# Summing a head's exponentials: the two halves of j added on GpSimd before TensorE sums them

## The chip, the core and the metric

The kernel runs on one core of a Trainium2 chip. The metric is the device time of that core in microseconds (us), the median of several runs. All data are fp32.

## The reference, cut to what matters

Two layers work on 64 graphs of 256 nodes with 256 features. Layer 0 is two graph attention layers, a layer norm, a feed-forward part and another layer norm. Layer 1 is a relational attention with 8 heads of 32 features, then a feed-forward part. The change touches only the attention of layer 1:

```
scores = einsum('bhid,bhjd->bhij', q, k) / sqrt(dh)
attn   = softmax(scores, axis=-1)              # over j
out    = sum over r of einsum('bhij,bhjd->bhid', attn * (adj == r), v_r)
```

Since adj holds only 0 and 1 here, the kernel uses the relations 0 and 1 alone. It computes exp(scores) without taking a maximum away, multiplies by the values, sums exp over j beside that, and divides at the end.

## The kernel before, in words

The 64 graphs are worked on as 32 pairs. `whole_way(pair)` is a generator that goes through the stages of one pair: `gat_layers`, `feed_forward` with Relu, `attention`, `feed_forward` with Gelu, and the store. `in_turn` (L151) drives three such generators at once while the program is written. At each `yield us, later, needs` it counts a planned time on, and picks the next generator that is due by it. So the order of the instructions on every engine is fixed when the program is built, by the planned costs in the yields; on the chip each engine works through its own queue in that order and waits on semaphores.

In `attention` (L345) a graph b of the pair and a half c of the features make a group: four heads (HQ = 4) of 32 features, 4 groups for a pair, n = 0 to 3. For a group:

- `scores` (L354) makes exp(scores) transposed: j lies on the partitions, in two halves jc of 128, and i along the columns. The four heads' products (L360) use four row strips of TensorE. One exp per head (L365, ScalarE) writes the tile `a`, 128 x 512, that holds jc = 0 in its first 256 columns and jc = 1 in the other 256.
- `of_relation_1` (L369) multiplies `a` by adj into `m` on VectorE (L374), four times. `m` has 6 buffers for the 4 in use.
- `sums` (L378) multiplies `ones` (128 x 32) with `a` on TensorE (L381): for each half jc and each head o, 256 columns, adding the two halves up in PSUM. Its result, the sum over j for each i, lies on 32 partitions a head, in columns 256 to 511 of the bank `po`.
- `products` (L384) does the same with the values, once with `a` (r = 0) and once with `m` (r = 1), into columns 0 to 255 of `po` (L388).
- `divided` (L392) takes the reciprocal of the sums (L394), a check value (L396), and multiplies into `oT` (L398), all on VectorE.

The loop is software-pipelined: a step n first issues the scores of group n + 1 on TensorE, then the sums and products of group n, then on VectorE the m of group n + 1 and the division of group n. Between steps `in_turn` places a step of another pair, in this stage one block of the feed-forward part (L308). After n = 1 the values of the second graph are made (L335, L337). After n = 2 `into_rows(0)` projects the first graph (L405) and follows with `add_rows` (L266) and `layernorm` (L273 to L282) on VectorE; `into_rows(1)` comes after n = 3, with L319 blocks of another pair ahead of it. The layer norm has one instruction on GpSimd, the power that makes rstd (L276). GpSimd also adds a bias to the rows (L292) while they are transposed (L289, L290). On VectorE, `most` of a coming pair's adj (L216) lies among these.

A matmul of this kernel shows as two records in the profile[...].

Of the kernel before, what the change touches and what calls it, by code (L numbers as in the profile page):

```python
# [10 lines left out]
F32 = mybir.dt.float32  # L11
# [4 lines left out]
ALU = mybir.AluOpType  # L16
AX = mybir.AxisListType

P = 128
# [10 lines left out]
def two_layers(ctx: ExitStack, tc: tile.TileContext, t: dict, out: bass.AP, flag: bass.AP):  # L30
# [9 lines left out]
    nc = tc.nc  # L40
    B, N, D = out.shape
# [6 lines left out]
    DH = D // H  # L48
    HQ = P // DH
# [25 lines left out]
    ones = const.tile([P, DH], F32, name="ones")  # L75
# [28 lines left out]
    with tc.tile_pool(name="setup", bufs=1) as setup, \  # L104
# [11 lines left out]
        for m in range(KC):  # L116
            pw = psetup.tile([P, 512], F32, name="pw")
            for c in range(KC):
                nc.tensor.matmul(pw[:, :D + 4], lhsT=w1T[:, c, m * P:(m + 1) * P], rhs=right[:, c],
                                 start=c == 0, stop=c == KC - 1)  # L120
# [17 lines left out]
    work = ctx.enter_context(tc.tile_pool(name="work", bufs=1))  # L138
# [3 lines left out]
    def bank():  # L142
        return psum.tile([P, 512], F32, name="ps")
# [30 lines left out]
    def done_with(name):  # L174
        del alone[name]

    def of_graph(b):
        return slice(2 * b, 2 * b + 2)
# [84 lines left out]
    def add_rows(y, p, b):  # L263

        rows = y[:, of_graph(b), :].rearrange("p k d -> p (k d)")
        nc.vector.tensor_tensor(rows, p, rows, ALU.add)  # L266

    def layernorm(r, gb, b):
        g, beta = gb
        st, mv = small.tile([P, 2, 6], F32, name="st"), small.tile([P, 2, 2], F32, name="mv")  # L270
        rstd = small.tile([P, 2], F32, name="rstd")
        for j in range(2):
            nc.vector.bn_stats(st[:, j, :], r[:, 2 * b + j, :])  # L273
            nc.vector.bn_aggr(mv[:, j, :], st[:, j, :])
        nc.vector.tensor_scalar(rstd, mv[:, :, 1], EPS, None, ALU.add)  # L275
        nc.gpsimd.tensor_tensor(rstd, rstd, mhalf[:, :2], ALU.pow)  # L276
        for j in range(2):
            row = r[:, 2 * b + j, :]
            nc.vector.scalar_tensor_tensor(row, row, mv[:, j, 0:1], g, op0=ALU.subtract, op1=ALU.mult)
        for j in range(2):  # L280
            row = r[:, 2 * b + j, :]
            nc.vector.scalar_tensor_tensor(row, row, rstd[:, j:j + 1], beta, op0=ALU.mult, op1=ALU.add)  # L282
# [11 lines left out]
    def rows_transposed(y, bias):  # L294
        yT = work.tile([P, KC, 512], F32, name="yT", bufs=2)
        for b in range(2):
            transposed(y, yT, bias, b)
            yield 0.5, 0.5 + b * 0.5, None
        return yT
# [31 lines left out]
    def values(v, jc, at, yT):  # L331

        ps = bank()
        for c in range(KC):
            nc.tensor.matmul(ps, lhsT=yT[:, c, at:at + P], rhs=wv[:, c].rearrange("p r m -> p (r m)"),  # L335
                             start=c == 0, stop=c == KC - 1)
        nc.vector.tensor_tensor(v[:, jc], ps, bv, ALU.add)  # L337

    def projected(to, c, yT, w, bias, scale):
        ps = bank()  # L340
        for d in range(KC):
            nc.tensor.matmul(ps, lhsT=w[:, d, c * P:(c + 1) * P], rhs=yT[:, d, :], start=d == 0, stop=d == KC - 1)  # L342
        nc.scalar.activation(to[:, c, :], ps, AF.Identity, bias=bias[:, c:c + 1], scale=scale)

    def attention(y, pair, adjT):  # L345


        yT = yield from rows_transposed(y, bo)
        qT, kT, oT = (work.tile([P, KC, 512], F32, name=n) for n in ("qT", "kT", "oT"))

        def values_tile():
            return work.tile([P, 2, 2 * D], F32, name="v", bufs=2)

        def scores(b, c):  # L354
            ps = [bank() for _ in range(HQ)]
            for jc in range(2):
                at = b * N + jc * P
                for o in range(HQ):
                    rows = slice(o * DH, (o + 1) * DH)
                    nc.tensor.matmul(ps[o][:, jc * N:(jc + 1) * N], lhsT=kT[rows, c, at:at + P],  # L360
                                     rhs=qT[rows, c, b * N:(b + 1) * N], start=True, stop=True)
            e = []
            for o in range(HQ):
                a = work.tile([P, 512], F32, name="a", bufs=2 * HQ)
                nc.scalar.activation(a, ps[o], AF.Exp)  # L365
                e.append(a)
            return e

        def of_relation_1(b, e):  # L369
            adj = adjT[:, of_graph(b), :].rearrange("p k n -> p (k n)")  # L370
            ms = []
            for a in e:
                m = work.tile([P, 512], F32, name="m", bufs=HQ + 2)
                nc.vector.tensor_tensor(m, a, adj, ALU.mult)  # L374
                ms.append(m)
            return ms

        def sums(e, po):  # L378
            for jc in range(2):
                for o in range(HQ):  # L380
                    nc.tensor.matmul(po[o * DH:(o + 1) * DH, N:], lhsT=ones, rhs=e[o][:, jc * N:(jc + 1) * N],  # L381
                                     start=jc == 0, stop=jc == 1)

        def products(c, r, v, ms, po):  # L384
            for jc in range(2):
                for o in range(HQ):
                    at = r * D + (c * HQ + o) * DH
                    nc.tensor.matmul(po[o * DH:(o + 1) * DH, :N], lhsT=v[:, jc, at:at + DH],  # L388
                                     rhs=ms[o][:, jc * N:(jc + 1) * N],
                                     start=r == 0 and jc == 0, stop=r == 1 and jc == 1)  # L390

        def divided(b, c, po):  # L392
            s = work.tile([P, N], F32, name="s", bufs=2)
            nc.vector.reciprocal(s, po[:, N:])  # L394
            junk = work.tile([P, N], F32, name="junk")
            nc.vector.scalar_tensor_tensor(junk, po[:, N:], 1.0, s, op0=ALU.mult, op1=ALU.add,  # L396
                                           accum_out=reach[:, pair, b * KC + c:b * KC + c + 1])
            nc.vector.tensor_tensor(oT[:, c, b * N:(b + 1) * N], po[:, :N], s, ALU.mult)  # L398

        def into_rows(b):  # L400
            ps = bank()
            for j in range(2):
                k = 2 * b + j
                for c in range(KC):
                    nc.tensor.matmul(ps[:, j * D:(j + 1) * D], lhsT=oT[:, c, k * P:(k + 1) * P], rhs=wo[:, c, :],  # L405
                                     start=c == 0, stop=c == KC - 1)
            add_rows(y, ps, b)
            layernorm(y, ln[2], b)

        groups = [(b, c) for b in range(2) for c in range(KC)]  # L410
        v = values_tile()
        projected(qT, 0, yT, wq, bqs, SCALE)
        projected(kT, 0, yT, wk, bk, 1.0)
        yield 3.44, 0.0, None
        values(v, 0, 0, yT)
        yield 1.72, 0.0, None
        e = scores(*groups[0])
        ms = of_relation_1(0, e)
        projected(qT, 1, yT, wq, bqs, SCALE)
        yield 3.0, 0.0, None  # L420
        projected(kT, 1, yT, wk, bk, 1.0)
        values(v, 1, P, yT)
        yield 3.44, 0.0, None
        for n, (b, c) in enumerate(groups):
            last = n == len(groups) - 1
            if not last:
                ahead = scores(*groups[n + 1])
            po = bank()
            sums(e, po)
            products(c, 0, v, e, po)  # L430
            products(c, 1, v, ms, po)
            if not last:
                e, ms = ahead, of_relation_1(groups[n + 1][0], ahead)
            divided(b, c, po)
            yield 3.1 if last else 4.1, 3.2 if last else 0.8, None
            if (b, c) == (0, KC - 1):
                v = values_tile()
                for jc in range(2):
                    values(v, jc, N + jc * P, yT)
                    yield 1.72, 0.0, None  # L440
            if n == 2:
                into_rows(0)
                yield 1.75, 0.0, None
        into_rows(1)
        done_with("attention")
        yield 1.75, 4.5, "ff"

    def whole_way(pair):
        yield 0.0, 0.0, "gat"
        xT, adjT, x = loaded.pop(pair)  # L450
        yield from gat_layers(pair, xT, adjT, x)
        yield from feed_forward(x, ff0, AF.Relu, ln[1])
        yield 3.44, 4.5, "attention"
        yield from attention(x, pair, adjT)
        yield from feed_forward(x, ff1, AF.Gelu, ln[3])
        nc.sync.dma_start(out[2 * pair:2 * pair + 2].rearrange("b (c p) d -> p (b c) d", p=P), x)
        yield 3.44, 0.0, None
# [439 lines left out]
```

## Time and profile before

| what | us |
|---|---|
| median of 3 runs (3450.34 to 3454.68) | 3452.26 |
| the profiled execution's own time | 3450.98 |
| its span | 3449.2 |
| TensorE busy | 3344.4 (97%) |
| VectorE busy | 1904.6 (55%) |
| ScalarE busy | 1371.0 (40%) |
| GpSimd busy | 481.5 (14%), of it 206.1 the power of rstd and 276.1 the bias adds |
| sums with ones (L381), 2048 records | 137.0, 385 ns each |
| products with values (L388), 4096 records | 267.8, 379 ns each |
| m (L374), 512 | 327.0, 688 ns by the page, 686 at the median |
| exp (L365), 512 | 264.4, 602 ns by the page |
| bias add on GpSimd (L292), 384 | 728 ns at the median of the first feed-forward's |

The span of the profiled execution is 1.8 us shorter than its own time; what lies around it is start and end of the program. Matmul records overlap: four that run side by side each show 379 ns, so the time that a block of matmuls takes is read from the start of one block to the start of the next, not from the sum of its records. The granted clock of TensorE is full almost throughout (0.999).

### The profile page before, as it was taken

To read this page: it belongs to the slowest core of one execution; us is meant where nothing else is said; L and a number is where in the kernel's file an instruction comes from. 1 tells how busy PE (TensorE), PEld (TensorE's weight loads), DVE (VectorE), ACT (ScalarE), POOL (GpSimd) and SP (SyncE) were. 2 spreads that over 40 slices of the span, in tenths; PEclk is the share of its full clock that TensorE was granted. 3 is DMA by queue.
4 is the path that set the end of the run, shared out by engine and by line. 5 is a ranking of instruction groups with operands and counts; after the bars stand their busy time and mean duration, and the time that the engine had idled before them with its cause. 6 is when DMAs were issued, how large, how long until landed. Compare 5 with 4: busy or idle time off the path is not lost.

```text
span 3449.2 us, 47284 instructions
## 1 busy us (share of the span) xinstructions
PE 3344.4 (97%) x18698; PEld 2150.5 (62%) x18698; DVE 1904.6 (55%) x4825; ACT 1371.0 (40%) x2586; POOL 481.5 (14%) x646
## 2 busy tenths in 40 slices
PE   7999999999999999999999999999999999999998
PEld 5566665666656566565665666656666566565655
DVE  5655645556456564555645555465554655546455
ACT  4343343433434334343444434444253442534332
POOL 0201111011110111111111111111111111111110
PEclk9999999999999999999999999999999999999999
DMA  5000010000100001000000100001000010000000
GB/s 166 7 25 19 13 37 7 25 19 13 37 7 25 25 7 37 7 28 23 20 25 7 41 10 25 19 7 43 7 25 19 7 43 7 25 19 1 13 1 14
DMA packets 66868, 78.22 MB, mean 23 GB/s; under 512 B 3280, under 2 KB 57680, under 8 KB 66640
## 3 DMA queue, kind: packets, MB, share of 16 engines
q1 hardware_dynamic: 66640, 75.13, 7.0%
q8 instruction: 150, 2.46, 0.3%
q14 instruction: 78, 0.64, 0.1%
HBM read 58.34 MB, written 16.78 MB: 22 GB/s over the span
## 4 chain that ended last, share of the span: by engine, by line
PE 87%; ACT 9%; DVE 2%; DMA 1%; issue 0%; SPq 0%; POOL 0%; POOLq 0%; DVEq 0%
PE ps L319 26%; PE ps L308 23%; PE ps L342 7%; PE ps L335 6%; PE ps L388 6%; PE ps L360 4%; PE ps L381 4%; PE ps L253 3%; PE ps L405 3%; ACT L189 2%; ACT yT L290 2%; PE ps L241 2%; PE ps L227 2%; PE ps L289 1%; ACT ff L311 1%; DVE e L206 1%
## 5 line engine op out<-in xcount | busy, mean ns | idle before, releaser
L276 POOL TENSOR_TENSOR rstd<-rstd,mhalf 128x2 f32<-128x2 f32 x256 | 206.1, 805 | 2729.3 <-DVE rstd L275 2713.4
L308 PE MATMUL ps<-yT,w_L_gnn_W 128*128 128x512 f32 x1024 | 482.7, 602 | 14.2 <-ACT yT L290 12.5
L308 PE MATMUL ps<-yT,w_L_gnn_w_ff 128*128 128x512 f32 x1024 | 482.5, 602 | 14.1 <-ACT yT L290 12.5
L319 PE MATMUL ps<-w_L_gnn_w_ff,ff 128*128 128x256 f32 x2048 | 450.2, 379 | 0.0
L319 PE MATMUL ps<-w_L_gnn_W,ff 128*128 128x256 f32 x2048 | 449.9, 379 | 0.0
L319 PEld LDWEIGHTS ps<-w_L_gnn_W,ff 128*128 128x128 f32 x2048 | 389.1, 190 | 66.6 <-issue 15.3
L319 PEld LDWEIGHTS ps<-w_L_gnn_w_ff,ff 128*128 128x128 f32 x2048 | 389.0, 190 | 66.0 <-issue 14.8
L374 DVE TENSOR_TENSOR m<-a,adjT 128x512 f32<-128x512 f32 x512 | 327.0, 688 | 175.6 <-ACT a L365 134.9
L266 DVE TENSOR_TENSOR x<-ps,x 128x512 f32<-128x512 f32 x256 | 176.1, 688 | 444.3 <-PE ps L319 330.7
L311 ACT ACTIVATE ff<-ps,c_L_gnn_b_ff 128x512 f32<-128x512 f32 x256 | 176.0, 687 | 448.2 <-PE ps L308 448.2
L365 ACT ACTIVATE a<-ps 128x512 f32<-128x512 f32 x512 | 264.4, 602 | 216.3 <-PE ps L360 216.1
L337 DVE TENSOR_TENSOR v<-ps,b_L_gnn_bv 128x512 f32<-128x512 f32 x128 | 88.1, 689 | 400.5 <-PE ps L335 400.5
L308 PEld LDWEIGHTS ps<-yT,w_L_gnn_W 128*128 128x128 f32 x1024 | 183.0, 190 | 199.2 <-issue 174.1
L308 PEld LDWEIGHTS ps<-yT,w_L_gnn_w_ff 128*128 128x128 f32 x1024 | 183.1, 190 | 198.9 <-issue 174.2
L290 ACT ACTIVATE yT<-ps 128x512 f32<-128x512 f32 x192 | 110.2, 592 | 479.8 <-PE ps L289 479.8
L311 ACT ACTIVATE ff<-ps,c_L_gnn_b 128x512 f32<-128x512 f32 x256 | 175.9, 687 | 292.8 <-PE ps L308 292.4
L335 PE MATMUL ps<-wv,yT 128*128 128x512 f32 x512 | 235.4, 592 | 0.0
L229 ACT ACTIVATE xw<-ps 128x260 f32<-128x260 f32 x128 | 45.7, 379 | 456.0 <-PE ps L227 456.0
L394 DVE RECIPROCAL s<-ps 128x256 f32<-128x256 f32 x128 | 224.0, 1750 | 0.0
L273 DVE BATCH_NORM_STATS2 st<-x 128x6 f32<-128x256 f32 x512 | 192.7, 418 | 8.6
L206 DVE SCALAR_TENSOR_TENSOR e<-ps,ratio,up 128x256 f32<-128x256 f32 x256 | 115.7, 475 | 141.2 <-ACT up L201 141.2
L335 PEld LDWEIGHTS ps<-wv,yT 128*128 128x128 f32 x512 | 97.3, 190 | 122.5 <-issue 122.2
(81 smaller groups left out, 4290.1 us busy)
## 6 DMA issues: line engine op xcount, KB each, us to landing
xT<-in_xT SPq DMA_DIRECT2D x32, 512.0 KB, 4.6
adjT<-in_adjT SPq DMA_DIRECT2D x32, 512.0 KB, 3.9
x<-in_x SPq DMA_DIRECT2D x32, 512.0 KB, 4.2
out<-x SPq DMA_DIRECT2D x32, 512.0 KB, 3.2
w_L_gnn_w_ff<-in_L_gnn_w_ff SPq DMA_DIRECT2D x2, 1024.0 KB, 11.3
w_L_gnn_W<-in_L_gnn_W SPq DMA_DIRECT2D x2, 1024.0 KB, 7.0
wv<-in_L_gnn_Wv SPq DMA_DIRECT2D x2, 256.0 KB, 7.1
w_L_gnn_W1T<-in_L_gnn_W1T SPq DMA_DIRECT2D x1, 256.0 KB, 6.1
```

The source lines that it names most:

```text
L273: nc.vector.bn_stats(st[:, j, :], r[:, 2 * b + j, :])
L276: nc.gpsimd.tensor_tensor(rstd, rstd, mhalf[:, :2], ALU.pow)
L290: nc.scalar.activation(yT[:, :, b * N:(b + 1) * N], pt.rearrange("p (c n) -> p c n", c=KC), AF.Copy)
L308: nc.tensor.matmul(p1, lhsT=w1[:, c, m * P:(m + 1) * P], rhs=yT[:, c, :], start=c == 0, stop=c == KC - 1)
L311: nc.scalar.activation(h, p1, func, bias=b1[:, m:m + 1])
L319: nc.tensor.matmul(p2[:, j * D:(j + 1) * D], lhsT=f[m][:, k * P:(k + 1) * P], rhs=w2[:, m, :], start=m == 0, stop=m == NF - 1)
L335: nc.tensor.matmul(ps, lhsT=yT[:, c, at:at + P], rhs=wv[:, c].rearrange("p r m -> p (r m)"), start=c == 0, stop=c == KC - 1)
L342: nc.tensor.matmul(ps, lhsT=w[:, d, c * P:(c + 1) * P], rhs=yT[:, d, :], start=d == 0, stop=d == KC - 1)
L365: nc.scalar.activation(a, ps[o], AF.Exp)
L374: nc.vector.tensor_tensor(m, a, adj, ALU.mult)
L388: nc.tensor.matmul(po[o * DH:(o + 1) * DH, :N], lhsT=v[:, jc, at:at + DH], rhs=ms[o][:, jc * N:(jc + 1) * N], start=r == 0 and jc == 0, st ...
L394: nc.vector.reciprocal(s, po[:, N:])
```

## The change

`halves_added` is new: for each head of a group one GpSimd instruction adds the two halves of `a`, columns 0 to 255 and 256 to 511, into a tile `halves` of 128 x 256 with 6 buffers. `sums` then multiplies `ones` with that tile, one product a head instead of two. `products` still uses `a` itself. The planned costs of the steps in the loop are 0.4 lower.

```diff
+        def halves_added(e):
+            hs = []
+            for a in e:
+                h = work.tile([P, N], F32, name="halves", bufs=HQ + 2)
+                nc.gpsimd.tensor_tensor(h, a[:, :N], a[:, N:], ALU.add)
+                hs.append(h)
+            return hs
...
-        def sums(e, po):
-            for jc in range(2):
-                for o in range(HQ):
-                    nc.tensor.matmul(po[o * DH:(o + 1) * DH, N:], lhsT=ones, rhs=e[o][:, jc * N:(jc + 1) * N],
-                                     start=jc == 0, stop=jc == 1)
+        def sums(hs, po):
+            for o in range(HQ):
+                nc.tensor.matmul(po[o * DH:(o + 1) * DH, N:], lhsT=ones, rhs=hs[o], start=True, stop=True)
...
         e = scores(*groups[0])
-        ms = of_relation_1(0, e)
+        hs, ms = halves_added(e), of_relation_1(0, e)
...
             po = bank()
-            sums(e, po)
+            sums(hs, po)
             products(c, 0, v, e, po)
             products(c, 1, v, ms, po)
             if not last:
-                e, ms = ahead, of_relation_1(groups[n + 1][0], ahead)
+                e, hs, ms = ahead, halves_added(ahead), of_relation_1(groups[n + 1][0], ahead)
             divided(b, c, po)
-            yield 3.1 if last else 4.1, 3.2 if last else 0.8, None
+            yield 2.7 if last else 3.7, 3.2 if last else 0.8, None
```

## The prediction

> **What bounds the kernel now.** I read the page's totals and chain first, then the attention stage by itself: a window table over it, the waits of TensorE in it, and the timelines of TensorE and VectorE side by side.
>
> ```profile
> PE 3344.4 (97%) x18698; PEld 2150.5 (62%) x18698; DVE 1904.6 (55%) x4825; ACT 1371.0 (40%) x2586; POOL 481.5 (14%) x646
> ...
> PE 87%; ACT 9%; DVE 2%; DMA 1%; issue 0%; SPq 0%; POOL 0%; POOLq 0%; DVEq 0%
> ```
>
> TensorE is busy 97% of the span and is 87% of the chain; GpSimd is idle for six sevenths of it. In the stage that is changed TensorE has no gap at all. The row of the window table below (columns: stretch, its length, busy time of each engine) is the attention of one pair:
>
> ```profile
> 1597.00:1640.00 43.00, 43.00 (x333) 22.66 (x332) 27.05 (x48) 14.33 (x25) 1.10 (x2) 1.00 0.05 14
> ```
>
> So time taken off TensorE here is worth its full length until another engine comes last. Which one that would be is read from the two timelines (start, length, instruction, count). TensorE first, the last group of scores of a pair to its second output projection (L405):
>
> ```profile
> 1687.70 1.15 PE L360 MATMUL ps<-qT,kT 32*128 32x256 f32 x16
> 1688.78 1.07 PE L381 MATMUL ps<-a,ones 128*32 128x256 f32 x16
> 1689.67 1.05 PE L388 MATMUL ps<-a,v 128*32 128x256 f32 x16
> 1690.53 1.05 PE L388 MATMUL ps<-m,v 128*32 128x256 f32 x16
> ...
> 1695.15 1.07 PE L381 MATMUL ps<-a,ones 128*32 128x256 f32 x16
> ...
> 1703.15 1.03 PE L405 MATMUL ps<-w_L_gnn_Wo,oT 128*128 128x256 f32 x4
> ```
>
> and VectorE in the same stretch:
>
> ```profile
> 1689.50 1.29 DVE L374 TENSOR_TENSOR m<-a,adjT 128x512 f32<-128x512 f32 x2 [0.99 <-ACT a L365]
> 1691.66 1.29 DVE L374 TENSOR_TENSOR m<-a,adjT 128x512 f32<-128x512 f32 x2 [0.87 <-PE ps L388]
> 1692.88 1.75 DVE L394 RECIPROCAL s<-ps 128x256 f32<-128x256 f32 x1
> ...
> 1695.35 0.68 DVE L266 TENSOR_TENSOR x<-ps,x 128x512 f32<-128x512 f32 x1
> ...
> 1700.46 1.75 DVE L394 RECIPROCAL s<-ps 128x256 f32<-128x256 f32 x1
> ...
> 1702.59 0.42 DVE L398 TENSOR_TENSOR oT<-ps,s 128x256 f32<-128x256 f32 x1
> ```
>
> From the masked products m at 1689.50 to the last oT at 1702.59 + 0.42 = 1703.01, VectorE works through a queue with hardly a hole: four m, the division of group 3 (n = 2), L266 with the layer norm, then the division of group 4 (n = 3). The L405 block that starts at 1703.15 needs that oT from its second product on (the weights are taken chunk by chunk), at 1703.15 + 0.43 = 1703.58. The slack is 0.57 us, and the same to within 0.2 us in the pairs from 2 to 27. This is the nearest thing to a second bound.
>
> **What the Trainium skill says.** "TensorE: Matmul & The Clock Gate", Part 3 (packing small matmuls): products with 32 output columns on different column strips run side by side. The trace agrees: L388's 16 records take 0.86 us from block to block, four waves of 0.215. "SBUF — State Buffer", Who interferes with whom: GpSimd uses VectorE's second port pair; a VectorE operation with two SBUF inputs and a GpSimd operation that reads SBUF exclude each other. The trace agrees (columns: shortest/median/longest ns):
>
> ```profile
> L279 DVE SCALAR_TENSOR_TENSOR x<-x,mv,b_L_gnn_g_ln x256: 465/474/1029, 36.6 to 3349.5; 128x256 f32<-128x256 f32 x128
> L292 POOL TENSOR_TENSOR x<-x,b_L_gnn_b_ff x128: 714/728/1042, 42.0 to 3285.8; 128x256 f32<-128x256 f32 x128
> ```
>
> L279 has two SBUF inputs; it takes 474 ns alone and up to 1029 beside L292; L292 stretches from 728 to about 920. Statistics and PSUM reads on VectorE keep their length beside L292. "GPSIMD Engine Reference", Elementwise, puts a two-input add at 2.6 cycles an element, an estimate of 555 ns for 256 elements before dispatch; L292, the same operation on the same size, takes 728, and I use that.
>
> **The change, part by part.**
>
> *Removed:* per group, 8 of the 16 records of the sums, two of their four waves: 2 x 0.215 = 0.43 us (the sums take 0.89 us from start to next start now, 0.46 after). 32 pairs x 4 groups x 0.43 = 55 us, on the path.
>
> *Order:* the built programs of both kernels have the same order on ScalarE and VectorE, and on TensorE but for one L308 product of the first pair that changes places with L405's. The planner's smaller costs (3.7 for 4.1) move nothing else, so table loads stay. On GpSimd the 16 adds of a pair stand together, between a rstd power ahead and a rstd power behind; the power behind belongs to L266's layer norm, after the adds are done. SP's queue is as before.
>
> *Added:* 512 adds x 0.728 = 373 us on GpSimd, which goes from 14% to about 25%: no bound as a sum. The new buffers (6 for 4 in use) wait on sums of the group before, which TensorE does directly after the scores: free.
>
> *The new wait:* sums, first of a group's products, now wait for four adds, not for four exps; behind them in TensorE's queue stand all products. The exps of a group end 0.49 us apart. m and adds start on the same exps and both read two SBUF operands, so they take turns. The price of a turn: at 93.87 two L282 (two SBUF inputs, 256 wide) and three L292 alternate, and the two L282 that take 0.88 together alone take 1.82; their ends, and so a turn, are 0.88 us apart. m is 512 wide, 688 ns against 420 for 256 (L374, L398), so a turn of m and add is 0.88 + 0.27 = 1.15 us. Counted from the first m (1.80 us after the scores start), the fourth m ends after 0.69 + 3 x 1.15 = 4.13 us, the fourth add about 0.6 later, at scores + 6.5.
>
> When are the sums due? Scores to sums is 7.50, 6.79, 10.23 and 7.44 us for a pair's four groups. All but the first lose one shortened block, 0.43 (the third two): due at 7.50, 6.36, 9.4 and 7.01. Only the second group is late, by about 0.2 us. 32 x 0.2 = 6 us.
>
> *VectorE's queue:* in the fourth group the fourth m now ends at 1689.50 - 1687.70 + 4.13 = 5.93 us after the scores, against 1692.95 - 1687.70 = 5.25 before. From there to oT is unbroken VectorE work, 1703.01 - 1692.95 = 10.06 us, so oT comes at 15.99. TensorE wants it at 1703.58 - 1687.70 - 2 x 0.43 = 15.02, since two shortened blocks lie between. With some 0.05 us for the semaphore, L405 waits 1.0 us. In the last four pairs, where no next pair's adjT is reduced on VectorE (L216, 1.22 us), the slack is 1.3 us larger, and it doesn't wait. So 28 x 1.0 = 28 us come back. The first division in the pair also ends about 1 us later; its oT has 6 us to spare at the first L405, but the values' additions (L337) behind it may come to the third group's products with nothing to spare: 0.1 us a pair, 3 us.
>
> *Sum:* -55 + 6 + 28 + 3 = -18 us from the profiled 3450.98 (span 3449.2). The median of the runs shown is 3452.26, 1.3 us above that; from it, 3434 us.
>
> *Bounds of the unknown.* How m and add share is not in this trace for 512-wide operands. Lower end, m passing undisturbed: the fourth m, held by m's buffers until the products before are done, gains the same 0.43 and ends at 4.8; L405 is then due within 0.1 us of oT, and the whole 55 us stays less 3 at most: 3400. Two m ahead of the first add: fourth m at 5.4, wait 0.5, 28 x 0.5 + 9 = 23 back: 3420. The add first: fourth m at 6.4, wait 1.5, no late sums: -55 + 42 + 3 = -10, 3442. Upper end, the add holding the port for its whole 0.73 us: next rivals. I take turns with m first: both are released by the same exp, and L292's 728 ns against L374's 688 for half the elements leaves GpSimd the longer way to its first read (a guess; no row shows a tie).
>
> **Rivals.**
>
> *Full gain.* Adds fall into VectorE's waits for exps and for m's buffers (0.9 us holes at 1689 and 1691), and into its divisions, which read PSUM. For it: TensorE at 43.00 of 43.00. Against it: the adds become ready with the m. 3398 to 3424.
>
> *Slower: the port is the bound.* Each add holds the port for all of its 0.73 us and m runs at its 0.60 pitch: a turn of 1.33. The fourth m then ends at 1.80 + 0.69 + 3 x 1.33 = 6.48, L405 waits 1.5 us; the second group's fourth add ends at 1.80 + 4 x 1.33 + 0.1 = 7.2 against 6.36, and TensorE stands 0.85 us at the sums. 28 x (2.35 - 1.73) + 4 x (0.85 - 1.73) = +14 us; 3466, to 3480 if the values come late too. It decides once the two waits of a pair exceed 1.73 us. For it: GpSimd's 728 ns and L279's 1029. Against it: L282/L292's turn of 0.88, shorter than 0.39 + 0.73.
>
> *No change:* a turn near 1.25, or the add first with some late sums: 3445 to 3459.
>
> **How the numbers follow.** Turns as computed, 3425 to 3445: 0.48. Full gain or nearly: 0.17. No change: 0.15. Slower: 0.20. Bounds at 0.2% of 3452 are 3445 and 3459 (about what a measurement of this kernel can tell from no change). Faster 0.65, same 0.15, slower 0.20. The range leaves out half of the first rival and half of the slower one: 3408 to 3466. Both signs are possible; the likeliest case alone is 3425 to 3445.
>
> **What would show it.** In the profile after: the sums at 0.46 us a block and with half of L381's 137 us busy; adds of 0.73 to 0.95 us on GpSimd; m with a mean above 688 ns, near 950; a new TensorE wait of about 1.0 us at L405 for oT in 28 pairs, and one of 0.2 us at the second group's sums for the adds. No wait at L405 and m at 688 would mean the full gain. It is wrong if the sums wait in groups other than the second, if the order of a turn is not one each, or if other stages move, which this working leaves alone.

## The result, and the profile after

| | median us | runs | ratio to before | 95% interval |
|---|---|---|---|---|
| before | 3454.22 | 6 (same chip) | 1 | |
| after | 3455.55 | 6 (3453.92 to 3457.52) | 1.0007 | 0.9994 to 1.0019 |

No change can be measured. The forecast was 3434; the range (3408 to 3466) holds the result, the direction does not. The profiled execution of after took 3456.74 us, its span is 3455.0, the clock 0.998.

In after, lines 369 onward are shifted: the adds are L373, m is L382, the sums L388, the products L394, the reciprocal L400, oT L404, and the output projection L411. These are the page's totals, its chain, and the groups of the adds and of m (busy us, mean ns, idle before):

```profile
PE 3320.8 (96%) x17674; PEld 2131.0 (62%) x17674; DVE 2090.0 (60%) x4825; ACT 1368.5 (40%) x2586; POOL 1066.6 (31%) x1158
...
PE 74%; DVE 11%; ACT 9%; issue 3%; DMA 1%; POOL 1%; SPq 0%; ACTq 0%; DVEq 0%; POOLq 0%
...
L373 POOL TENSOR_TENSOR halves<-a 128x256 f32<-128x256 f32 x512 | 576.2, 1154 | 483.4 <-ACT a L365 483.4
L382 DVE TENSOR_TENSOR m<-a,adjT 128x512 f32<-128x512 f32 x512 | 517.9, 1070 | 104.3 <-ACT a L365 104.0
```

TensorE is 74% of the chain, not 87%, and VectorE 11%, not 2%. VectorE has the same 4825 instructions and is busy 185 us longer; m alone takes 191 us more, at 1070 ns each against 688. The adds take 1154 ns, where the same operation alone takes 728. So both engines pay for working at once. A stretch like the one shown of before, the attention of a pair beside a Relu feed-forward:

```profile
1602.00:1646.00 44.00, 43.27 (x308) 22.82 (x307) 32.58 (x48) 14.33 (x25) 19.02 (x18) 1.00 0.04 13
```

TensorE now stands still for 0.73 us in it, and VectorE works 32.6 of 44 us where it worked 27.1 of 43. The hole is in the waits of TensorE (total, times, longest us), where the projection had one wait of 0.2 us before:

```profile
PE ps L411 <- DVE oT L404: 28.7, 28, 1.5
```

Between the steps of a pair's attention stands the feed-forward part of another pair. It is the one with Relu in 16 pairs and the one with Gelu in the other 16, and the two kinds come out differently.

*A pair beside Relu.* TensorE's timeline, last sums to the projection:

```profile
1635.61 0.64 PE L388 MATMUL ps<-halves,ones 128*32 128x256 f32 x8
1636.07 1.05 PE L394 MATMUL ps<-a,v 128*32 128x256 f32 x16
...
1643.18 0.59 PE L411 MATMUL ps<-w_L_gnn_Wo,oT 128*128 128x256 f32 x2
1644.51 1.56 PE L411 MATMUL ps<-w_L_gnn_Wo,oT 128*128 128x256 f32 x6 [0.73 <-DVE oT L404]
```

The sums take 0.46 us from start to start (1635.61 to 1636.07), 0.43 less than before, and the projection waits for the last oT. Setting each block of after (its start to the start of the next) against the same block of before gives for the four groups -0.43, -0.22, -0.43 and -0.43, and +1.00 at the projection: -0.52 us a pair. The other pairs of this kind up to pair 26 show the same, with +0.99 to +1.20 at the projection. That is the working of the prediction to the tenth, the 0.2 of the second group included.

*A pair beside Gelu.* The same comparison gives -0.10, -0.43, -0.16, +0.12, and +1.56 (+1.44 to +1.77 in the pairs of this kind from 3 to 27): +1.0 us a pair, where -0.5 was expected. The first cause is on ScalarE, at the first exps of the pair. Before (timelines of ScalarE and TensorE):

```profile
1665.51 1.28 ACT L365 ACT_TABLE_LOAD   x1
1666.41 1.15 PE L360 MATMUL ps<-qT,kT 32*128 32x256 f32 x16
1667.58 2.06 ACT L365 ACTIVATE a<-ps 128x512 f32<-128x512 f32 x4 [0.78 <-PE ps L360]
```

and after:

```profile
1671.13 1.15 PE L360 MATMUL ps<-qT,kT 32*128 32x256 f32 x16
1672.33 1.28 ACT L365 ACT_TABLE_LOAD   x1 [2.12 <-PE ps L360]
1673.62 2.06 ACT L365 ACTIVATE a<-ps 128x512 f32<-128x512 f32 x4
```

Gelu and exp alternate on ScalarE, and each change costs a table load of 1.28 us (three before exps in each of 16 pairs; none beside Relu). Before, the load began 0.9 us ahead of the scores and was done when they were. After, it begins only when the scores are there: the exps start 2.49 us behind the start of the scores, not 1.17. The built programs show why:

```
before:  L365 LoadActFuncSet [waits DVE]       L365 Activation a<-ps [waits PE]
after:   L365 LoadActFuncSet [waits DVE,PE]    L365 Activation a<-ps [waits Pool]
```

The exp overwrites a buffer of `a` that was read by VectorE (m) and is now read by GpSimd (the add) too. So it has one more wait. In both built programs no operation of ScalarE carries more than one wait of its own; what else it must wait for stands on a waiting instruction ahead of it, and the table load stands between the two. With the wait on GpSimd on the exp, the wait for the scores has moved ahead of the load. The operations stand in the same order as before; only the waits differ.

So what remained open was whether this late load, the sharing of VectorE and GpSimd, or both, cost the expected 18 us, and what the change would give without them.

### The profile page after: what moved, and what is told of

Same layout as the page of the kernel before. It is cut to its first block, busy times and chain, and to the rows that moved or that the text cites. A ratio compares the mean times of both kernels' runs of the same rounds, so it can differ in the third digit from the quotient of the medians.

```text
span 3455.0 us, 46095 instructions
## 1 busy us (share of the span) xinstructions
PE 3320.8 (96%) x17674; PEld 2131.0 (62%) x17674; DVE 2090.0 (60%) x4825; ACT 1368.5 (40%) x2586; POOL 1066.6 (31%) x1158
## 4 chain that ended last, share of the span: by engine, by line
PE 74%; DVE 11%; ACT 9%; issue 3%; DMA 1%; POOL 1%; SPq 0%; ACTq 0%; DVEq 0%; POOLq 0%
PE ps L319 23%; PE ps L308 20%; PE ps L342 7%; PE ps L335 5%; PE ps L394 4%; PE ps L360 3%; PE ps L253 3%; DVE s L400 3%; DVE m L382 2%; ACT L189 2%; ACT yT L290 2%; PE ps L241 2%; PE ps L227 2%; PE ps L411 2%; PE ps L388 1%
## 5 line engine op out<-in xcount | busy, mean ns | idle before, releaser
L276 POOL TENSOR_TENSOR rstd<-rstd,mhalf 128x2 f32<-128x2 f32 x256 | 215.4, 841 | 1666.3 <-DVE rstd L275 1652.2
L373 POOL TENSOR_TENSOR halves<-a 128x256 f32<-128x256 f32 x512 | 576.2, 1154 | 483.4 <-ACT a L365 483.4
L382 DVE TENSOR_TENSOR m<-a,adjT 128x512 f32<-128x512 f32 x512 | 517.9, 1070 | 104.3 <-ACT a L365 104.0
L319 PE MATMUL ps<-w_L_gnn_w_ff,ff 128*128 128x256 f32 x2048 | 450.2, 379 | 0.0
L319 PE MATMUL ps<-w_L_gnn_W,ff 128*128 128x256 f32 x2048 | 449.9, 379 | 0.0
L319 PEld LDWEIGHTS ps<-w_L_gnn_W,ff 128*128 128x128 f32 x2048 | 390.0, 190 | 65.7 <-issue 15.3
L319 PEld LDWEIGHTS ps<-w_L_gnn_w_ff,ff 128*128 128x128 f32 x2048 | 389.8, 190 | 65.2 <-issue 14.8
L337 DVE TENSOR_TENSOR v<-ps,b_L_gnn_bv 128x512 f32<-128x512 f32 x128 | 84.9, 684 | 308.6 <-PE ps L335 308.6
L400 DVE RECIPROCAL s<-ps 128x256 f32<-128x256 f32 x128 | 223.5, 1746 | 0.0
```

The lines of the kernel that those rows point to most:

```text
L319: nc.tensor.matmul(p2[:, j * D:(j + 1) * D], lhsT=f[m][:, k * P:(k + 1) * P], rhs=w2[:, m, :], start=m == 0, stop=m == NF - 1)
L373: nc.gpsimd.tensor_tensor(h, a[:, :N], a[:, N:], ALU.add)
```

## The experiments

The theory: the 55 us of TensorE are saved; m and adds delay VectorE by turns (the oT of the last group is late at L411), and in the Gelu pairs late table loads delay it further. The rival: the table loads alone, or GpSimd's sharing alone, is the whole of it. Each ratio is to before run beside it. Where the time of a single part is wanted, medians are compared; those of before itself lie from 3451.5 to 3454.6 us, so a difference of medians is good to about 3 us.

**e1: early table loads.** One small ScalarE operation stands behind the exps of the coming group, reads the last `halves` of the present group, and so takes the wait on GpSimd ahead of the next exps. The loads again wait on VectorE only.

```diff
                 ahead = scores(*groups[n + 1])
+                touched = small.tile([P, 1], F32, name="touched")
+                nc.scalar.activation(touched, hs[-1][:, :1], AF.Identity, bias=ahead[-1][:, :1])
```

> The changed kernel with one tiny ScalarE operation more in each step, which reads the last halves tile of the group just before. ScalarE has then seen GpSimd's semaphore, so an exp that writes over a tile that GpSimd read needs no wait on GpSimd of its own, and the wait for the scores no longer stands ahead of the table load of the exps beside Gelu. Theory (late table loads): in the 16 pairs whose attention runs beside Gelu the loads start before the scores again and these pairs behave like those beside Relu, which gain 0.5 us each where the Gelu ones lose 1.0: 16 x 1.5 = 24 us less than the changed kernel, about 3431 against 3455; the waits at the second output projection (some 1.0 us in 28 pairs) stay. Rival (the Gelu pairs lose because VectorE and GpSimd share the port there with more work): the loads move, but the time stays within 5 us of 3455.

Measured: 3441.75 us, 0.9967 [0.9955, 0.9979]. In its timeline the load is back ahead of the scores:

```profile
1662.63 1.28 ACT L365 ACT_TABLE_LOAD   x1
1663.54 1.15 PE L360 MATMUL ps<-qT,kT 32*128 32x256 f32 x16
1664.70 2.06 ACT L365 ACTIVATE a<-ps 128x512 f32<-128x512 f32 x4 [0.78 <-PE ps L360]
```

That gives 13.8 us back, not the 24 expected; by the two traces the 16 Gelu pairs get 12.7 (0.6 to 1.0 each; in the pair compared +1.0 becomes +0.06 us). A Gelu pair still doesn't reach -0.52: its third group gains 0.11 instead of 0.43, and its projection comes 1.26 us later where that of a Relu pair comes 0.95 later. Both go with the values of the second graph (L337), which come late behind the division and stand ahead of the last m: these begin 2.13 us after their scores, not 1.80 as in before. The late loads are a good half of the loss against the forecast, and not all that goes back.

**e2: projection later.** The planned cost behind a pair's last group is raised, so that one more L319 block (3.45 us) of another pair stands ahead of L411. The addition and the layer norm behind the projection move back with it on VectorE.

```diff
-            yield 2.7 if last else 3.7, 3.2 if last else 0.8, None
+            yield 2.7 if last else 3.7, 6.6 if last else 0.8, None
```

> The changed kernel with the second output projection of each pair planned later (6.6 for 3.2), which puts one more block of 16 second feed-forward products ahead of it on TensorE. Theory (the division on VectorE comes last at that projection): the wait there, 28.7 us in 28 places, goes, and nothing takes its place: about 3427. Rival (the wait only moves, since layer norm and transposes behind the projection come later by the same 3.4 us): 3450 or more, with a new wait at the transposes. The late table loads stay in this kernel.

Measured: 3419.25 us, 0.9900 [0.9885, 0.9915]. The wait at L411 is gone from the list, and the time is 36 us lower: the list counts holes of 0.73 and 1.29 us a pair, 28.7 together, while the blocks behind them come 1.00 and 1.56 us later, 14 x 2.56 = 36. The groups beside Gelu keep their -0.10, -0.43, -0.16, +0.12.

**e3: both.** The edits of e1 and e2 together.

> The changed kernel with both edits, the tiny ScalarE operation and the later projection. Theory: what the late loads cost at the sums and at the values goes (about 1 us in each of 16 pairs, 15 us) and so does all of the wait at the projection (28.7 us): about 3411, 43 us below both kernels. If the two causes overlap more, up to 3425. If neither is a cause, 3455.

Measured: 3410.26 us, 0.9875 [0.9860, 0.9890]. With the projection out of the way the early loads are still worth 9 us.

**e4: half the sums, no adds.** `sums` takes the first half of `a` itself (the other half of j is left out of the denominator), and GpSimd adds nothing.

```diff
-                h = work.tile([P, N], F32, name="halves", bufs=HQ + 2)
-                nc.gpsimd.tensor_tensor(h, a[:, :N], a[:, N:], ALU.add)
-                hs.append(h)
+                hs.append(a[:, :N])
```

> The changed kernel without the GpSimd adds: the sums with ones take the first half of each exp alone, so that the second half of j is left out of the softmax's denominator. It is the saving on TensorE by itself. Theory: 128 x 0.43 = 55 us off the kernel before, 3398 to 3402, since without adds VectorE's m keep 690 ns and the last oT is there within 0.1 us of the second output projection. Rival (another bound lies close behind TensorE whatever the adds do): above 3415, with waits of TensorE at that projection of 0.3 us or more a pair.

Measured: 3399.33 us, 0.9844 [0.9829, 0.9859]. All groups show -0.43. So the saving on TensorE is the 55 us of the working, and all of what is lost goes to how the sums over the halves are made.

**e5: adds whose result isn't used.** Before with the GpSimd adds put in; the sums stay as they were.

```diff
+        def halves_added(e):
+            for a in e:
+                h = work.tile([P, N], F32, name="halves", bufs=HQ + 2)
+                nc.gpsimd.tensor_tensor(h, a[:, :N], a[:, N:], ALU.add)
...
+                halves_added(ahead)
```

> The kernel before with the GpSimd adds put beside it and their result unused: the sums with ones keep all of their products. It is the cost of the adds with nothing saved. Theory (sharing the port and late table loads together): m takes turns with the adds, near 1.13 us each; beside Relu the last oT comes 0.7 us later against a slack of 0.5, a wait of 0.2 us a pair at the second output projection; beside Gelu the exps come another 1.3 us later, a wait of about 1.5 us a pair: 14 x 0.2 + 14 x 1.5 = 24 us, about 3478. Rival (the adds are hidden while TensorE has its full work): within 5 us of 3454.

Measured: 3487.14 us, 1.0097 [1.0080, 1.0114]. The excess over the expectation comes from three Gelu pairs that lose 4.1 to 4.7 us. One of them (the DMA queue, VectorE, TensorE in its timeline, then the DMA view of 635 to 642 us: packets, MB and share, and us from issue to landing):

```profile
635.51 0.37 SPq L61 DMA_DIRECT2D adjT<-in_adjT  x1
...
641.67 1.22 DVE L216 TENSOR_REDUCE most<-adjT 128x4 f32<-128x1024 uint32 x1 [2.25 <-DMA adjT<-in_adjT]
...
647.82 2.51 PE L410 MATMUL ps<-w_L_gnn_Wo,oT 128*128 128x256 f32 x6 [3.51 <-DVE oT L403]
...
q8 instruction: 1, 0.02, 0.8%
...
adjT<-in_adjT SPq DMA_DIRECT2D x1, 512.0 KB, 6.1
```

A coming pair's adjT is loaded into the buffer that the pair's m have read. The load starts 0.03 us behind the last m, in before too, and lands some 3.9 us later, just when VectorE comes to L216. Here it took 6.1 us, and L216 waits for it with the division of the last group queued behind. In all of the late loads of e5 and e12 the fetch of an instruction page (queue q8) lies among the packets; others with such a fetch landed in time, so that it is a likely cause and not a shown one. TensorE then stands for 3.51 us, and its next six records take 2.51 us where they take 1.56 elsewhere: the clock record shows half speed for 3.4 us from there.

**e8: the wait alone.** As e5, but each add is of one column, so that the exps have the wait on GpSimd and GpSimd hardly reads.

```diff
-                nc.gpsimd.tensor_tensor(h, a[:, :N], a[:, N:], ALU.add)
+                nc.gpsimd.tensor_tensor(h, a[:, :1], a[:, N:N + 1], ALU.add)
```

> The kernel before with four tiny GpSimd adds of one column per group in place of adds of 256, results unused: exps get the wait on GpSimd, and so their table loads beside Gelu come after the wait for the scores, but GpSimd hardly uses the port. Theory: the exps of those pairs come 1.2 us later, and that alone is hidden: the fourth m of a pair's last group ends 0.35 us later, under the slack of 0.5 us; 3452 to 3458. Rival (the late loads cost by themselves, about 1 us in each of 16 pairs): 3468 or more.

Measured: 3453.76 us, 1.0002 [0.9993, 1.0011]. The loads are late in its trace as in after, with the scores of this one from 1669.39 on, and no block of the pairs compared moves:

```profile
1670.59 1.28 ACT L365 ACT_TABLE_LOAD   x1 [2.12 <-PE ps L360]
```

**e9: adds, early loads.** As e5 with the small operation of e1.

> The kernel before with the full adds, unused, and with the tiny ScalarE operation that gets the table loads early again: sharing the port alone, nothing saved. Theory: a wait of 0.2 us a pair at the second output projection beside Relu and up to 0.5 beside Gelu: 4 to 10 us above before, 3458 to 3464. Rival (the port is what costs, the loads nothing): the same as with the adds unused and loads late.

Measured: 3457.93 us, 1.0018 [1.0011, 1.0025].

**e10: before with the later projection** (3.2 to 6.6).

> The kernel before with the second output projection planned later (6.6 for 3.2) and no other edit. Theory: nothing waits at that projection there, so the place is worth nothing by itself: within 5 us of 3454. Rival (the later place helps any kernel, by a better order): 10 us or more below before, and then the gain of that edit in the changed kernel is no proof of a wait of its making.

Measured: 3453.29 us, 1.0000 [0.9991, 1.0009]. The kernel before has nothing to win there.

The four together settle the rival. By their ratios, late loads alone cost nothing that can be measured, adds alone 6 us (0.0018 x 3452), both 33 (0.0097 x 3452). The two delays add up in VectorE's queue: each alone stays within or near the slack of half a microsecond at the projection, together they pass it. In the pairs compared the projection comes 0.29 (Relu) and 0.15 us (Gelu) later with adds alone, 0.22 and 1.51 with both.

**e11: sums last.** e3 with the sums behind the products in three of the four groups.

```diff
             po = bank()
-            sums(hs, po)
+            if n == 2:
+                sums(hs, po)
             products(c, 0, v, e, po)
             products(c, 1, v, ms, po)
+            if n != 2:
+                sums(hs, po)
```

> The changed kernel with both mends (early table loads by a small ScalarE operation, projection later by 6.6), and with the sums of groups 1, 2 and 4 behind their products in TensorE's queue in place of ahead of them; in the third group they stay ahead. My theory: the sums' wait for the adds in the second group (0.2 us in 32 pairs, 6 to 7 us) goes, since products of 1.7 us stand ahead of them; m of the same group is ready in time. 3403 to 3406 against 3410 with both mends. Rival: the wait only changes its name, because the products with m come 0.46 us earlier and wait for the fourth m, or the division starts late: 3410 or more.

Measured: 3407.07 us, 0.9866 [0.9851, 0.9881], some 3 below e3 and 1 above the expectation. The interval overlaps that of e3, so the difference rests on the traces. The late sums of the second group are gone: all groups beside Relu show -0.43. Beside Gelu, the third group shows +0.09 in place of e3's -0.10, and by 0.52 us in 16 pairs, 8 us, this one place is the distance to e4.

**e7: adds on VectorE, projection later.** The edit of e2, and the other engine:

```diff
-                nc.gpsimd.tensor_tensor(h, a[:, :N], a[:, N:], ALU.add)
+                nc.vector.tensor_tensor(h, a[:, :N], a[:, N:], ALU.add)
```

> The changed kernel with the adds of halves on VectorE, ahead of the m of their group, in place of GpSimd, and with the planned cost behind a pair's last group at 6.6, so that the second output projection stands behind one more block. The exps keep the waits that put the table loads behind the scores. My theory: next to m the adds cost VectorE as much from GpSimd (turns of 1.13 us for an m and an add) as they would if it did them itself (0.69 + 0.42 = 1.11 us), and GpSimd only delays the adds. Then VectorE's queue comes out as before, the sums in the second group wait less (up to 0.2 us in 32 pairs, 6 us), and the time is that of the later projection alone or a little less: 3411 to 3421. Rival: GpSimd takes real work off VectorE; then about 0.25 us a group more on VectorE, the projection waits again, and the time is above 3425.

Measured: 3399.39 us, 0.9839 [0.9825, 0.9852]. That is e4 with the right result: nothing is lost, in either kind of pair, and it is 20 us below e2, which differs in the engine of the adds alone. The table loads stay late all the while, though no GpSimd operation reads `a` here: in the built program the exp's further wait is then on ScalarE's own semaphore (behind 47 of the 48 loads), and the wait for the scores again stands ahead of the load. I had expected 3411 to 3421, so my reading of what an add costs was wrong. VectorE's timeline of a group:

```profile
1657.39 0.43 DVE L373 TENSOR_TENSOR halves<-a 128x256 f32<-128x256 f32 x1 [0.25 <-ACT a L365]
1657.73 0.69 DVE L382 TENSOR_TENSOR m<-a,adjT 128x512 f32<-128x512 f32 x1
1658.34 1.09 DVE L373 TENSOR_TENSOR halves<-a 128x256 f32<-128x256 f32 x3
1659.34 1.89 DVE L382 TENSOR_TENSOR m<-a,adjT 128x512 f32<-128x512 f32 x3
1661.14 1.75 DVE L400 RECIPROCAL s<-ps 128x256 f32<-128x256 f32 x1
```

Instructions on one engine overlap at their ends: three adds take 1.09 us, (1.09 - 0.43) / 2 = 0.33 each from start to start, and three m 1.89, 0.60 each. I had added their full durations (0.69 + 0.42 = 1.11). Eight of them take 1661.14 - 1657.39 = 3.75 us; in after the four m alone take 4.02 to the next instruction:

```profile
1695.01 4.10 DVE L382 TENSOR_TENSOR m<-a,adjT 128x512 f32<-128x512 f32 x4 [0.96 <-ACT a L365]
1699.03 1.74 DVE L400 RECIPROCAL s<-ps 128x256 f32<-128x256 f32 x1
```

So VectorE does the adds itself in less time than it loses to GpSimd's, and they are done earlier.

**e12: adds on VectorE alone.** After with only that one edit; the projection stays.

> The changed kernel with one edit: the adds of halves on VectorE in place of GpSimd. The projection stands where it stood, and the exps keep the waits that put the table loads behind the scores. From the trace of the run with the adds on VectorE and a later projection: TensorE loses no time there (3399), the last oT of a pair ends at 1616.62 us in a pair beside Relu and would be due at 1619.06 - 3.45 + 0.43 = 1616.04, and at 1680.01 beside Gelu against 1681.03 - 3.45 + 0.43 = 1678.01. My theory: without the later projection these waits of 0.6 and 2.0 us come back in 14 pairs each, 3399 + 37 = 3436 (3430 to 3442), some 20 us faster than the changed kernel, since an add costs VectorE 0.34 us of its own against the 0.53 by which a GpSimd add lengthens the turn of an m. Rival: beside m it is all the same which engine adds; then the time is that of the changed kernel, 3455, or no more than the late sums' 6 us below it.

Measured: 3451.48 us, 0.9992 [0.9984, 1.0000], 13 runs from 3443.66 to 3452.40. The gain is less than expected: 4 us against after, with intervals that overlap. The steps are as worked out in most pairs: all groups -0.43, the projection +0.73 beside Relu and +2.0 beside Gelu. But in five Gelu pairs more is lost, together some 12 us. The largest, in the timelines of VectorE and TensorE:

```profile
1270.96 1.22 DVE L216 TENSOR_REDUCE most<-adjT 128x4 f32<-128x1024 uint32 x1 [1.82 <-DMA adjT<-in_adjT]
...
1277.10 2.93 PE L411 MATMUL ps<-w_L_gnn_Wo,oT 128*128 128x256 f32 x6 [3.36 <-DVE oT L404]
```

and as a window behind that wait (columns as above; the clock is third from the end):

```profile
1278.00:1286.00 8.00, 8.00 (x27) 6.59 (x27) 4.45 (x13) 0.00 (x0) 0.79 (x1) 0.70 0.00 0
```

The clock is 0.70 in these 8 us. The clock record has a stretch of half speed in each of the five pairs, of 3.41 us in four and of 6.83 in this one, and each microsecond of it loses half: 20.5 / 2 = 10 of the 12 us. They follow waits of 1.85 to 3.4 us; two other pairs with waits of 1.86 and 1.87 kept their full clock. The mean clock of the execution is 0.995, against 0.998 in after. In two of the five pairs adjT lands late as in e5 (L216 waits for it for 1.82 and 1.12 us, in the other Gelu pairs for 0.15 to 0.43). The expectation had left out both.

**e13: adds on VectorE, early loads,** the projection where it stood.

> The adds of halves on VectorE, the table loads made early again by the small ScalarE operation, and the projection where it stood. My theory: the exps beside Gelu come 1.28 us earlier, and so does the last oT there; its wait falls from 2.0 to 0.7 us, that of the Relu pairs stays at 0.6: 3399 + 14 x 1.3 = 3417 (3411 to 3424). Rival: the loads are hidden by another wait of VectorE (for a coming pair's adjacency, 0.34 us in the trace), and less than half of the 18 us comes.

Measured: 3419.36 us, 0.9905 [0.9890, 0.9920]. Here the early loads are worth 32 us against e12, 35 by the two profiled executions: 14 x (2.0 - 0.9) = 15 from the waits themselves, 12 in the five pairs, where no late adjT and no stretch of half clock comes any more, and 4 in the start-up, which has one such stretch here and two in e12. The start-up differs from one execution to the next. What is left is in the list of waits:

```profile
PE ps L411 <- DVE oT L404: 15.4, 28, 1.1
```

Its pairs show -1.73 in the groups and +0.74 (Relu) or +0.90 (Gelu) at the projection.

## Why the prediction was wrong, point by point

- *Removed, 55 us:* right. e4 and e7 both stand 55 us below before.
- *The turn of m and add, 1.15 us:* right. Four m take 4.10 us, (4.10 - 0.69) / 3 = 1.14; the Trainium skill's page "SBUF — State Buffer", section Who interferes with whom, led to this, and the trace agrees that both engines pay. The turn is shorter than an m and an add one behind the other (0.60 + 0.73 = 1.33), so the two don't exclude each other over their whole length. The single operations show longer than forecast, 1154 ns for the adds and 1070 for m on average, against 0.73 to 0.95 us and 950 ns: a record covers the other engine's part of the turn. What I didn't ask is how that compares with VectorE doing the add, 0.60 + 0.33 = 0.93 a turn.
- *Late sums, 0.2 us in the second group:* right beside Relu (0.21); e11 takes it away. Beside Gelu the waits fall into the first, third and fourth group.
- *L405 waits 1.0 us in 28 pairs:* right in 14, 1.56 in the other 14; the wait list's 28.7 us in 28 pairs looks like a hit, but it counts the holes (0.73 and 1.29 us) and not the delays behind them (1.00 and 1.56), as e2 showed; that the sum fits is luck.
- *Values, 0.1 us a pair:* too small beside Gelu, where the third group loses about 0.3, also in e1 where the loads are early; beside Relu nothing is lost.
- *"The planner's smaller costs (3.7 for 4.1) move nothing else, so table loads stay":* **this is the step that failed.** I compared the order of the instructions and took equal order for equal time. I named the new waits of TensorE and the new buffers, but not that GpSimd became a reader of `a`, so that each exp has one wait more before it overwrites it. That moved the wait for the scores ahead of the table load, and the exps of 16 pairs started 1.3 us later. It isn't peculiar to GpSimd: with the adds on VectorE (e7) the loads are as late.

The sum with the Gelu pairs as they are: the forecast's Gelu pairs were -0.5 us and became +1.0, 14 x 1.5 = 21 us, and -18 + 21 = +3, which is where after stands (1.3, interval -2 to +7). e1 takes 13.8 of the 21 back. The other 7 are two sizes beside Gelu: the values' additions in the third group (0.3 us a pair in e1) and the projection (0.3 to 0.4 beyond that of a Relu pair). I had written that the slack at L405 is the same in all pairs, and in before it was. The timelines of the working at 1687 to 1703 us are those of a Gelu pair, but with its loads still hidden; the due times of the sums were those of a Relu pair. So one set of numbers stood for both kinds.

None of my rivals described this. "No change" was given 0.15 for a longer turn or the add going first; the time came out there by another way. "Slower" needed a turn of 1.33, and there was none.

Not shown: why, of an exp's waits, the one for the scores is moved ahead of the load when there is one wait more. Only that it is, 48 times in after, and that the small operation of e1 undoes it.

## What to carry to other kernels

When a change gives a buffer a new reader, on another engine (after) or on one that read it before (e7), look at who overwrites that buffer: its wait list can grow, and the order of instructions doesn't show where the waits end up. Work out an engine's share with the pitch from start to start, and ask what the idle engine costs the busy one: here the add cost VectorE 0.54 us (1.14 - 0.60) when GpSimd did it and 0.33 when VectorE did. And once the path has a slack of half a microsecond, delays that are nearly harmless one at a time are priced together: 0 for the late loads, 6 for the adds, 33 for both; moving the consumer one block later (36 us) was worth more here than taking away the late loads alone (14).

## What the runs showed of the hardware that I had not expected

- A table load stands behind the waits it is given: with the wait for the scores on it, its 1.28 us, hidden before, lie open (exps 2.49 us after the start of the scores against 1.17).
- A TensorE wait can cost more than its length: after holes of 1.85 to 3.5 us at the projection the clock was at half in stretches of 3.4 us (once 6.8), in five Gelu pairs of e12 and three of e5. Holes of up to 1.5 us there in after led to none. The same length (1.85, 1.86) came with it and without. All these stretches of one trace start at whole multiples of 3.413 us from each other (in e12 1275.89 and 2132.64 us are 251 x 3.413 apart, in e5 648.28 and 1511.86 are 253 x 3.413), so the clock is changed at fixed instants, and where a hole lies may count beside its length: one of 1.88 us at 1916.41 in e12, which such an instant cuts into 1.19 and 0.69, kept the clock. Where the limit lies isn't shown: 1.85 us between two instants (2344.85) lost it, 1.86 and 1.87 between two (422.65, 1060.87) kept it.
- The start-up has such stretches too, and not the same in each execution: one of 3.4 us in before, 6.8 and 3.4 in after. In the two profiles the pairs begin 2 us apart for it.
